# Which partitions four reads fill, and which keys a block transpose takes, in the wide cross attentions of a decoder kernel

## The chip, the cores and the metric

The kernel runs on one core of one Trainium2 chip. The time is the device time of one execution in microseconds (us). Three runs of the kernel before took 2110.76, 2118.01 and 2122.07 us; the median is 2118.01 us.

A core has five engines that run side by side, each with its own instruction queue: TensorE (PE in the profile; PEld is its weight loads), VectorE (DVE), ScalarE (ACT), GpSimd (POOL) and SyncE (SP), which here only issues DMA transfers. 16 DMA engines move the data of all queues. Working memory on the core has 128 partitions (rows); matrix products come out in eight banks.

## The reference

Four layers of a decoder over x of 4 batches, 256 tokens and 128 features, with a context of 512 tokens and 96 features. Each layer is self-attention, cross-attention and a feed-forward part. The change touches two of these twelve parts, the cross-attentions of the first and the last layer, with 16 heads of 64 features each:

```python
q = query @ w_q                      # 256 tokens x 1024
k, v = jnp.split(context @ w_kv, 2, axis=-1)   # 512 keys x 1024 each
scores = jnp.einsum('bhqd,bhkd->bhqk', q, k) * SCALE
attn = jax.nn.softmax(scores, axis=-1)
out = jnp.einsum('bhqk,bhkd->bhqd', attn, v)
return out.reshape(B, NQ, INNER) @ w_out + b_out
```

The first layer's version adds low-rank terms to the weights and treats the last 4 of the 512 context tokens apart. All is in 32-bit floats.

## The kernel before

The kernel calls the twelve parts by short names; X0 and X3 are the two cross-attentions, and F3, the last feed-forward part, is a local-attention network of six layers that fills the time from about 1,270 us on. Work of neighbouring parts is interleaved: the profile's stretches from 30 to 395 us and from 936 to 1270 us hold X0 and X3 with pieces of their neighbours.

Most of the order is not written out by hand. Every piece of work is registered with `op(name, ...)` under a name with an engine, a duration and a due time (a table, `NET`, with `"p_turn": ("DVE", 1.17, -1794.64)` among others), and with the buffers that it reads and writes. A planner (`Flow.order`) then plays the program through once with these numbers, at build time, and fixes the order of the instructions on every engine. On the chip each engine keeps to that order and waits, where it must, on semaphores. The numbers of the table are constants in the source.

X0 and X3 are made by `cross_wide` (lines 637 to 659) and `cross_pair` (661 to 724). A pair is two heads; there are 8 pairs in each of 4 batches, so 32 pairs in X0 and 32 in X3. For one pair:

- PE makes the keys (64 features of two heads by 512) and the queries, then, for each of two blocks of 128 queries, the scores of both heads: two banks of 128 queries x 512 keys (`p_scores`).
- DVE takes the row maximum of each (line 690), ACT the exponential with the row sum (line 692), DVE the reciprocal (line 694), POOL multiplies (line 697). The probabilities of a block lie in a tile `p` of 128 queries x 1024 (two heads x 512 keys).
- To weigh the values, PE needs the probabilities turned: keys on the partitions. This is done in two steps. First DVE transposes blocks of 32 x 32 inside `p` into a tile `ts` of 128 x 2048 (line 730, `blocks_turned`, name `p_turn`; once for each block of queries, so twice a pair). After it, partitions 32a to 32a + 31 hold, for the 32 queries of group a, the 32 keys of each block, one key to a partition.
- Second, the blocks have to come from the four groups of 32 partitions into their right places. `blocks_moved` (lines 735 to 745) sends `ts` to a room in HBM with one DMA of 1 MB (line 744, `p_send`, 128 rows of 8 KB) and reads it back with four DMAs of 256 KB (line 742, `p_move`), each of which collects from all four query groups what belongs to one quarter `m` of the key positions, in rows of 2 KB, and fills 32 partitions of the tile `pT`. Send and reads are issued by SP. SP waits for the turns before the send and for the landing of the send before the reads.
- PE multiplies with the values (`p_weigh`, line 718) and ACT copies the result out.

There are three rooms, two `ts`, two `pT` and three `p` tiles. SP also issues the fetches of weights (line 429) from the same queue, in the planned order. X0 differs in one thing that is seen in the profile: 508 keys are taken for the maxima and exponentials, and 4 are treated apart (line 707).

The key numbers of a block of 128 keys run from 0 to 127, and `pT` has key number n of a block on partition n.

Of the kernel before, what the change touches and what calls it, by code (L numbers as in the profile page):

```python
# [346 lines left out]
class Net:  # L347
# [378 lines left out]
    def blocks_turned(self, p, ts, t, reads):  # L726


        nc, done = self.nc, Buffer()
        self.op("p_turn", lambda: nc.vector.transpose(  # L730
            ts.t.rearrange("p (m t x i) -> p t m x i", m=4, t=2, i=32)[:, t],
            p.t.rearrange("p (x m i) -> p m x i", m=4, i=32)), reads, [done], [p, ts])
        return done

    def blocks_moved(self, ts, turned, pT):

        nc, room, sent = self.nc, self.fixed("room", self.rooms), Buffer()

        def move():
            from_, to = room.t.rearrange("(a j) (m x) -> m j a x", a=4, m=4), pT.t.rearrange("p (a x) -> p a x", a=4)  # L740
            for m in range(4):
                nc.sync.dma_start(out=to[32 * m : 32 * (m + 1)], in_=from_[m])

        self.op("p_send", lambda: nc.sync.dma_start(out=room.t, in_=ts.t), turned, [sent], [ts, room])
        self.op("p_move", move, [sent], [pT], [room])
# [2014 lines left out]
```

## Time and profile before

| | |
|---|---|
| time of the three runs | 2110.76, 2118.01, 2122.07 us |
| the profiled execution's own time | 2115.48 us |
| its span, first to last instruction | 2113.8 us |
| granted TensorE clock, mean | 0.974 of full speed |
| turns on DVE, line 730 | 128 of 1233 ns, 157.1 us |
| sends, line 744 | 64 of 1024 KB, 7.2 us from issue to landing (median) |
| reads, line 742 | 256 of 256 KB, 6.9 us from issue to landing (median) |
| DMA bytes in the whole run | 205.34 MB, of which sends and reads make 64 x 2 MB |

The page shows one execution. "Busy" is the time in which an engine works on an instruction; the rest is idle, and for every idle stretch the profile names what ended it ("PE bank L412 <- DMA arena<-room" is PE, at line 412, waiting for a transfer from a room into the working memory, whose name is `arena`). The chain is the sequence of work that ended last, followed back from the last instruction; only what lies on it sets the time directly. A table of stretches gives each engine's busy time in a piece of the span, the granted clock, the share of time for which the DMA engines were busy and the bytes that they moved.

### The profile page before, as it was taken

To read this page: it belongs to the slowest core of one execution; us is meant where nothing else is said; L and a number is where in the kernel's file an instruction comes from. 1 tells how busy PE (TensorE), PEld (TensorE's weight loads), DVE (VectorE), ACT (ScalarE), POOL (GpSimd) and SP (SyncE) were. 2 spreads that over 40 slices of the span, in tenths; PEclk is the share of its full clock that TensorE was granted. 3 is DMA by queue.
4 is the path that set the end of the run, shared out by engine and by line. 5 is a ranking of instruction groups with operands and counts; after the bars stand their busy time and mean duration, and the time that the engine had idled before them with its cause. 6 is when DMAs were issued, how large, how long until landed. Compare 5 with 4: busy or idle time off the path is not lost.

```text
span 2113.8 us, 58090 instructions
## 1 busy us (share of the span) xinstructions
PE 1974.5 (93%) x23506; PEld 1273.4 (60%) x23511; DVE 1659.4 (79%) x4177; ACT 1145.2 (54%) x2642; POOL 991.1 (47%) x1155
## 2 busy tenths in 40 slices
PE   9889999999999998998979889999999999999998
PEld 5445565766666675654544446666666666666566
DVE  6776877778775769898878579798798797987883
ACT  4554545254547676765536454555555556555553
POOL 4334334241221245544354355567476565674670
PEclk9999999999999999999989899999999999999999
DMA  5886828501100000029487872112112121021110
GB/s 162 235 252 197 234 77 243 161 21 45 69 9 9 1 1 26 25 66 249 126 209 238 234 215 82 42 32 84 31 53 72 32 63 52 24 83 33 29 43 22
DMA packets 79403, 205.34 MB, mean 97 GB/s; under 512 B 10648, under 2 KB 23008, under 8 KB 70944
## 3 DMA queue, kind: packets, MB, share of 16 engines
q1 hardware_dynamic: 66896, 185.72, 31.1%
q10 hardware_dynamic: 12240, 15.91, 2.5%
q8 instruction: 186, 3.05, 0.6%
q14 instruction: 81, 0.66, 0.1%
HBM read 108.80 MB, written 67.63 MB: 83 GB/s over the span
## 4 chain that ended last, share of the span: by engine, by line
PE 47%; DVE 26%; DMA 12%; POOL 7%; issue 4%; ACT 3%; SPq 1%; POOLq 0%; DVEq 0%; ACTq 0%
PE bank L412 30%; PE bank L1858 10%; DMA arena<-room 5%; DMA room<-arena 4%; PE bank L415 3%; DVE arena L2012 3%; POOL arena L2064 3%; DVE arena L2022 3%; DVE arena L2027 3%; PE bank L2074 2%; DVE arena L730 1%; DVE arena L2103 1%; DVE arena L2117 1%; DVE arena L690 1%; POOL arena L2026 1%
## 5 line engine op out<-in xcount | busy, mean ns | idle before, releaser
L412 PE MATMUL bank<-arena 128*128 128x128 f32 (+11 forms) x6824 | 884.0, 402 | 77.9 <-DMA arena<-room 55.4
L412 PEld LDWEIGHTS bank<-arena 32*128 32x128 f32 (+5 forms) x6824 | 543.0, 168 | 365.6 <-issue 152.1
L1858 PE MATMUL bank<-arena 64*64 64x32 f32 (+2 forms) x13584 | 648.2, 251 | 9.8 <-issue 4.9
L1858 PEld LDWEIGHTS bank<-arena 64*64 64x64 f32 (+2 forms) x13584 | 385.7, 127 | 207.1 <-issue 136.9
L420 ACT COPY arena<-bank 128x256 f32<-128x256 f32 (+4 forms) x498 | 223.4, 472 | 327.0 <-PE bank L412 273.2
L697 POOL TENSOR_SCALAR arena<-arena 128x508 f32<-128x508 f32 (+1 forms) x256 | 177.6, 701 | 229.2 <-DVE arena L694 223.9
L2026 POOL TENSOR_TENSOR arena<-arena 128x1024 f32<-128x1024 f32 x96 | 226.0, 2363 | 49.1 <-DVE arena L2012 46.9
L2064 POOL TENSOR_TENSOR arena<-arena 128x1024 f32<-128x1024 f32 x96 | 181.5, 1905 | 87.9 <-DVE arena L2048 87.9
L692 ACT ACTIVATE arena<-bank,arena 128x508 f32<-128x508 f32 (+1 forms) x256 | 173.8, 688 | 83.1 <-DVE arena L690 54.2
L690 DVE TENSOR_REDUCE arena<-bank 128x1 f32<-128x508 f32 (+1 forms) x256 | 164.2, 673 | 32.9 <-PE bank L412 32.8
L2107 POOL TENSOR_TENSOR arena<-arena 128x1024 f32<-128x1024 f32 x48 | 91.4, 1903 | 178.8 <-DVE arena L2104 153.7
L2022 DVE TENSOR_TENSOR arena<-bank,arena 128x512 f32<-128x512 f32 x192 | 127.3, 682 | 55.7 <-ACT arena L2020 50.6
L730 DVE STREAM_TRANSPOSE arena<-arena 128x1024 f32<-128x1024 f32 x128 | 157.1, 1233 | 17.5 <-DMA room<-arena 9.3
L1007 ACT ACTIVATE arena<-bank 128x512 f32<-128x512 f32 (+1 forms) x256 | 125.1, 579 | 66.1 <-PE bank L412 65.3
L2020 ACT ACTIVATE arena<-bank 128x512 f32<-128x512 f32 x192 | 111.5, 598 | 73.2 <-PE bank L1858 51.8
L415 PE MATMUL bank<-ident,arena 128*128 128x128 f32 (+2 forms) x733 | 125.9, 289 | 18.5 <-POOL arena L1656 4.9
L2012 DVE TENSOR_TENSOR arena<-bank,arena 128x256 f32<-128x256 f32 x384 | 138.2, 414 | 5.7 <-ACT arena L2020 5.1
L984 DVE TENSOR_REDUCE arena<-bank 128x1 f32<-128x512 f32 (+2 forms) x256 | 115.5, 516 | 34.0 <-PE bank L412 33.7
L415 PEld LDWEIGHTS bank<-ident,arena 128*128 128x128 f32 (+2 forms) x733 | 83.4, 143 | 80.8 <-issue 21.8
L2080 ACT COPY arena<-bank 128x512 f32<-128x512 f32 x192 | 105.2, 611 | 43.1 <-PE bank L2074 42.6
L2074 PE MATMUL bank<-ident,arena 128*128 128x128 f32 x768 | 105.0, 279 | 15.2 <-POOL arena L2064 15.2
L449 POOL TENSOR_TENSOR arena<-arena,neghalf 128x2 f32<-128x2 f32 (+1 forms) x56 | 42.9, 772 | 156.8 <-DVE arena L448 153.2
(229 smaller groups left out, 2524.8 us busy)
## 6 DMA issues: line engine op xcount, KB each, us to landing
room<-arena SPq DMA_DIRECT2D x64, 1024.0 KB, 7.2
arena<-room SPq DMA_DIRECT2D x256, 256.0 KB, 6.9
arena<-arena SPq DMA_DIRECT2D x48, 384.0 KB, 3.4
arena<-in_f_w SPq DMA_DIRECT2D x24, 512.0 KB, 5.9
arena<-in_f_wqkv ACTq DMA_DIRECT2D x18, 512.0 KB, 4.3
arena<-arena SPq DMA_DIRECT2D x48, 128.0 KB, 2.4
arena<-in_f_wo ACTq DMA_DIRECT2D x6, 512.0 KB, 4.3
arena<-in_f_w ACTq DMA_DIRECT2D x6, 341.0 KB, 3.0
```

The source lines that it names most:

```text
L412: self.nc.tensor.matmul(out, lhsT, rhs, start=start, stop=stop)
L415: self.nc.tensor.transpose(out, in_, self.d.ident)
L420: return self.op(name, lambda: copy(out(), in_()), reads, writes, holds)
L690: self.op("p_max", lambda ps=ps, one=one: nc.vector.tensor_reduce(one(nmx), ps.t[:, :n], AX.X, ALU.max, negate=True), [ps], [most], [nmx])
L692: self.op("p_exp", lambda ps=ps, one=one, cols=cols: nc.scalar.activation(cols(), ps.t[:, :n], AF.Exp, bias=one(nmx), accum_out=one(sums)) ...
L697: nc.gpsimd.tensor_scalar(cols(), cols(), one(sums), 1.0, ALU.mult, ALU.mult)
L730: self.op("p_turn", lambda: nc.vector.transpose(ts.t.rearrange("p (m t x i) -> p t m x i", m=4, t=2, i=32)[:, t], p.t.rearrange("p (x m i) ...
L1858: self.nc.tensor.matmul(out, lhsT, rhs, start=start, stop=stop)
L2012: nc.vector.tensor_mul(heads(tmp.t[:, cut])[:, :, lo : lo + 32], heads(ps.t)[:, :, 32 - lo : 64 - lo], spread(1, lo, lo + 32),)
L2022: op("cosine", lambda cut=cut, ps=ps: nc.vector.tensor_mul(heads(out.t[:, cut]), heads(ps.t), spread(0, 0, 64)), [ps, w["tab"]], [out])
L2026: op("rotary", lambda: nc.gpsimd.tensor_add(out.t, out.t, tmp.t), [out, tmp], [out])
L2064: nc.gpsimd.tensor_mul(heads(out.t), heads(out.t), rs.t[:, at : at + 16, None].to_broadcast([P, 16, 64]))
```

## The change

Within each block of 128 keys, key number n used to be written as n = 32 m + i, with m from 0 to 3 and i from 0 to 31. A 32 x 32 block transpose took the 32 neighbouring keys of one m, and read m went to the 32 neighbouring partitions 32 m to 32 m + 31. The change writes n = 4 j + m. A block transpose takes the 32 keys m, m + 4, m + 8 and so on, so its input is read at a step of four elements, and read m fills the partitions m, m + 4, m + 8 and so on up to m + 124. The tile `ts`, the room and the finished `pT` keep their shapes, and `pT` holds the same numbers in the same places. Counts, bytes and rows of the transfers are the same, and the planner's table is unchanged.

```diff
@@ blocks_turned
         self.op("p_turn", lambda: nc.vector.transpose(
             ts.t.rearrange("p (m t x i) -> p t m x i", m=4, t=2, i=32)[:, t],
-            p.t.rearrange("p (x m i) -> p m x i", m=4, i=32)), reads, [done], [p, ts])
+            p.t.rearrange("p (x j m) -> p m x j", m=4, j=32)), reads, [done], [p, ts])
@@ blocks_moved
             from_, to = room.t.rearrange("(a j) (m x) -> m j a x", a=4, m=4), pT.t.rearrange("p (a x) -> p a x", a=4)
             for m in range(4):
-                nc.sync.dma_start(out=to[32 * m : 32 * (m + 1)], in_=from_[m])
+                nc.sync.dma_start(out=to[m::4], in_=from_[m])
```

## The prediction

> **What bounds the kernel now.** I read the page first: its busy shares, the chain of work that ended last, and the DMA row of the slices.
>
> ```profile
> span 2113.8 us, 58090 instructions
> PE 1974.5 (93%) x23506; PEld 1273.4 (60%) x23511; DVE 1659.4 (79%) x4177; ACT 1145.2 (54%) x2642; POOL 991.1 (47%) x1155
> ...
> DMA  5886828501100000029487872112112121021110
> ...
> PE 47%; DVE 26%; DMA 12%; POOL 7%; issue 4%; ACT 3%; SPq 1%; POOLq 0%; DVEq 0%; ACTq 0%
> PE bank L412 30%; PE bank L1858 10%; DMA arena<-room 5%; DMA room<-arena 4%; PE bank L415 3%; DVE arena L2012 3%; POOL arena L2064 3%; DVE arena L2022 3%; DVE arena L2027 3%; PE bank L2074 2%; DVE arena L730 1%; DVE arena L2103 1%; DVE arena L2117 1%; DVE arena L690 1%; POOL arena L2026 1%
> ```
>
> TensorE is busy for 93%, but that average is not the answer: the DMA row is high in two places only. These are the two stages in which the change's instructions run. The table of stretches, cut at those stages (X0 from 30 to 395 us, X3 from 936 to 1270 us), shows who has room there. Columns: the stretch, busy us of each engine with its count of instructions, granted TensorE clock, DMA share, GB/s.
>
> ```profile
> core 0: us, PE busy (x) PEld busy (x) DVE busy (x) ACT busy (x) POOL busy (x), PEclk, DMA share, GB/s
> 30.00:395.00 365.00, 334.92 (x2117) 201.92 (x2115) 280.27 (x820) 182.74 (x498) 135.05 (x344) 0.96 0.72 204
> 936.00:1270.00 334.00, 287.26 (x1459) 153.90 (x1458) 260.44 (x581) 173.62 (x461) 152.89 (x187) 0.92 0.76 212
> ...
> 936.00:1000.00 64.00, 55.97 (x275) 28.27 (x271) 57.61 (x137) 36.58 (x103) 27.61 (x35) 0.95 0.89 247
> 350.00:400.00 50.00, 49.57 (x389) 36.78 (x389) 44.49 (x120) 14.29 (x39) 12.84 (x28) 1.00 0.87 219
> ```
>
> VectorE (DVE) is idle for 85 us of X0 and 74 us of X3: that is all the room a longer DVE instruction has there. Then two short stretches around one pair that had the DMA engines to itself: in the first only its send was moving, in the second nearly only its four reads. The SyncE timeline gives their issues.
>
> ```profile
> 1031.80:1034.40 2.60, 2.60 (x11) 1.11 (x8) 2.53 (x10) 1.48 (x5) 1.01 (x2) 1.00 0.93 384
> 1035.90:1041.70 5.80, 5.80 (x19) 1.79 (x17) 5.73 (x15) 4.89 (x14) 2.73 (x4) 1.00 0.97 232
> ```
> ```profile
> 1030.94 0.34 SPq L744 DMA_DIRECT2D room<-arena  x1
> 1034.93 1.73 SPq L742 DMA_DIRECT2D arena<-room  x4
> ```
>
> Same 1 MB, same queue, engines full both times (0.93 and 0.97), but the send to 128 neighbouring rows runs at 384 GB/s and the reads into 32 neighbouring partitions each at 232. Last, the rows of the turn and of the waits for the reads, from the answers for the line and the room:
>
> ```profile
> L730 DVE STREAM_TRANSPOSE arena<-arena x128: 1197/1235/1248, 36.9 to 1251.9; 128x1024 f32<-128x1024 f32 x128
> ```
> ```profile
> L742 SPq DMA_DIRECT2D arena<-room x256: 302/430/1622, 43.5 to 1270.0; - x128
> ...
>   PE bank L412: 57.3, 25
>   PEld bank L412: 11.1, 3
> ```
>
> TensorE stood still 28 times, 68.4 us in all, for a read that had not landed.
>
> **Part 1, the turns (line 730 to 732).** 128 of them, two a pair, same count and same output; only the input is now read four elements apart. Nothing in this trace shows DVE reading f32 from SBUF at such a stride. The full rate is known: reductions on line 984 take 683 ns for 512 elements and 284 ns for 128, so (683 - 284)/384 = 1.04 ns an element, and 1024 x 1.04 = 1.06 us of the turn's 1.233 us are elements. The low end is therefore +0: the turn already runs at one element per step and cannot gain. The high end: one more step for every element, +1.06 us, a turn of 2.30 us. I take the high end. Neither row decides; my reason is that the old pattern brings four wanted values in each 16 bytes and the new one brings one, so a reader that fetches more than 4 bytes at a time loses its neighbours. It is a choice, and its opposite is the first rival.
>
> [...]
>
> So DVE gets 128 x 1.06 = 136 us more work: 64 turns in X0, 280 + 68 = 348 us in a stage of 365; 63 in X3, 260 + 67 = 327 us in one of 334. Filled to 95% and 98%, DVE would bind both. It can't be packed that tightly, since its instructions wait in a fixed order for PE, ACT and POOL: in the two fullest long stretches with many turns it reaches 57.6/64 = 90% and 44.5/50 = 89%. At 90% X0 takes 348/0.90 = 387 us (+22) and X3 327/0.90 = 363 us (+29 to +30): **+52 us**. At 95% it would be +1.5 and +10 (**+12**), at 85% +45 and +51 (**+96**). What is late next: behind a turn on DVE stand the next pair's row maxima (line 690), for which ACT's exponentials wait (54.2 us today, "ACT arena L692 <- DVE arena L690"), which hold the banks that PE needs; and on SyncE the send behind the turn (185.5 us, "SPq L744 <- DVE arena L730"), with every later send and weight fetch behind it in that queue. The order of all engines is planned ahead from a weight for the turn that the change leaves alone, so nothing is rearranged for a longer turn. Between the stages DVE has 425 of 541 us busy but PE 523, so PE's delay isn't won back there.
>
> **Part 2, the four reads (line 742).** Same count, bytes and 2 KB rows, same place in SyncE's queue; 64 x 4 issues at 0.43 us stay as they are. Only the partitions written change. Ends: nothing gained (232 GB/s as now; 219 was the slowest such stretch, which would lose 0.3 us), and the send's 384 GB/s, the only row with the same bytes over all 128 partitions. 1.05 MB take 4.5 us at 232 and 2.7 at 384: -1.8 us a pair. I take that, being the nearest row in which the partitions are spread. A read lands 6.9 us after its issue (median), so 1.8 is 26%; of the 68.4 us for which PE stood waiting that is **-18 us**. The idle time of the turn's other side, send and fetches, shares the same engines and gains a little; I count it with the 90%.
>
> [...]
>
> **Sum**, against the profiled execution's own 2115.48 us (2.5 us below the median of the runs, inside their spread of 2110.8 to 2122.1): +52 - 18 = +34, so 2149.5, say **2150 us**, 1.5% slower. This case's own range runs from +12 - 18 to +96 with no help from the reads: 2110 to 2211.
>
> **The rivals.** 0.5%, about 10.6 us, is what a measurement of this kernel can tell from no change.
> 1. *The stride is free* (ends on the other side): turns stay at 1.233 us, the reads gain. [...] Gain: at least the 18 us. At most, all DMA time on the chain shrinks: in X0 the chain is 26% DMA of rooms (95 us), in X3 33% (111 us); the reads save 1.8 of a pair's 4.5 + 2.7 us, 25%, so 51 us. Midway: -35, **2080 us** (2064 to 2097). It decides if the turn's mean stays below about 1.5 us: with +0.27 us a turn DVE stays at 82% and 83% in the two stages.
> [...]
> 3. *The stride costs far more*, three extra steps an element, +3.2 us a turn: X0 (280 + 204)/0.9 = 538, X3 (260 + 201)/0.9 = 512: +351, **2467 us**. Nothing in the trace speaks for it but that a reciprocal (line 2104: 253 ns for 16 elements, 145 for one on line 694) shows 7 ns an element is possible.
> 4. *Neither price moves*: same rate in both, **2116 us**.
>
> **How the numbers follow.** Forecast 58%, rival 1 20%, rival 2 12%, rival 3 5%, rival 4 5%. The range must reach into rival 1: from 2075 to 2211 it leaves out rival 3, somewhat under half of rival 1 and the forecast's tails, some 17%. Faster by over 0.5%: nearly all of rival 1 and a few per cent of the forecast, 22%; within 0.5%: rival 4 and the low side of the forecast, 16%; slower 62%.
>
> **What would show it.** The turn's row (near 2.30 us, or 1.23); GB/s in a stretch with one pair's reads alone (near 384, or 232) and their landing (near 5 us, or 6.9); DVE's busy time in the two stages (near 348 and 327 us) and its idle time; PE's waits for reads (near 50 us). The part of the chain on lines 730 and 690 should grow and that of the reads shrink. The prediction is wrong if the turns keep their time, if PE's slack takes 136 us of DVE work without the stages growing, or if the reads' gain in a DMA-full stretch outweighs DVE there.

## The result, and the profile after

The changed kernel takes 2507.2 us (median of four runs, 2501.5 to 2507.8) against 2114.4 us for the kernel before on the same chip (four runs, 2108.0 to 2122.1): 1.185 times as long, with a 95% interval of 1.180 to 1.190. I had forecast 2150 us and a range of 2075 to 2211. The sign was right, the size and the cause were not. One execution of kernel F below took 3212.7 us at a granted clock of 0.603, against 2074.6 to 2084.6 us in its four others, and F's numbers leave it out. The profiled execution of the changed kernel has a span of 2504.7 us, and the instructions stand in the same order on every engine as before.

First the page of the changed kernel: instructions, busy time, the DMA row of the slices, the share of the DMA queue, and the shares of the chain that ended last, by engine.

```profile
span 2504.7 us, 58273 instructions
PE 2088.8 (83%) x23511; PEld 1313.6 (52%) x23511; DVE 1754.4 (70%) x4177; ACT 1144.1 (46%) x2642; POOL 988.4 (39%) x1155
...
DMA  4444342431110000104234244422121212111110
...
q1 hardware_dynamic: 66896, 185.72, 22.2%
...
PE 35%; DVE 31%; DMA 13%; POOL 7%; issue 5%; SPq 4%; ACT 2%; DVEq 0%; POOLq 0%; ACTq 0%
...
L730 DVE STREAM_TRANSPOSE arena<-arena 128x1024 f32<-128x1024 f32 x128 | 257.0, 2018 | 230.1 <-DMA arena<-room 213.4
...
arena<-room SPq DMA_DIRECT2D x256, 256.0 KB, 4.0
```

The rows of the queue and of the turn on the page before the change were:

```profile
q1 hardware_dynamic: 66896, 185.72, 31.1%
...
L730 DVE STREAM_TRANSPOSE arena<-arena 128x1024 f32<-128x1024 f32 x128 | 157.1, 1233 | 17.5 <-DMA room<-arena 9.3
```

Two things in the new page are what the prediction spoke of. A turn takes 2018 ns instead of 1233, 99.9 us more for the 128 of them, and DVE as a whole has 95 us more work (1754.4 against 1659.4). And the DMA engines need less time for the same 185.72 MB: 22.2% of 2504.7 us is 556 us, where 31.1% of 2113.8 was 657, so 101 us less, 1.6 us a pair. The third is new and far larger: just before the turns DVE stood still for 230.1 us, 213.4 of them until *reads from a room* had landed. Before the change that idle time was 17.5 us and no turn waited for a read. A turn doesn't use what a read brings; it reads `p` and writes `ts`, and the reads fill `pT`. There are 183 more instructions, although the program asks for the same work. Five are matmuls that the earlier trace lacks (23,506 against 23,511); counted in the two traces, the other 178 are semaphore instructions: 96 more on DVE, 53 on SyncE, 29 on the other three. The first line below is the turn's semaphore line before the change, the two after it the turn's answer in the changed kernel (durations in ns: least, median, most):

```profile
L730 DVEq EVENT_SEMAPHORE  x70: 21/21/50, 48.3 to 1248.0; - x70
```
```profile
L730 DVE STREAM_TRANSPOSE arena<-arena x128: 1944/2014/2162, 36.5 to 1639.5; 128x1024 f32<-128x1024 f32 x128
L730 DVEq EVENT_SEMAPHORE  x123: 21/50/6816, 48.1 to 1628.7; - x123
```

Before there were 70 of these semaphore instructions, none longer than 50 ns; now there are 123, and one lasts 6816 ns. Then, in the answer for the reads' line of the changed kernel, who waited for the reads (us in total, times):

```profile
L742 SPq DMA_DIRECT2D arena<-room x256: 577/604/1298, 48.7 to 1649.6; - x128
...
  DVE arena L730: 213.4, 34
  DVE arena L448: 63.7, 8
  ACT arena L2080: 23.5, 2
  POOL arena L2064: 21.0, 3
  DVE arena L918: 19.3, 3
...
  PE bank L412: 18.3, 7
```

Before, only TensorE waited for the reads (57.3 and 11.1 us in the lines of the prediction), apart from one wait of 0.8 us on GpSimd. Now it stands seventh: the turns wait most, and so do the statistics of a norm (line 448) and lines of the local-attention network (2064, 2080) whose data have nothing to do with a room. It goes the other way too. These are SyncE's waits, in us in total, times, and the longest, first one before the change and then two in the changed kernel:

```profile
SPq L744 <- DMA arena<-room: 53.4, 36, 5.9
```
```profile
SPq L744 <- DMA arena<-room: 161.7, 80, 5.4
...
SPq L742 <- DVE arena L694: 80.0, 12, 10.5
```

The reads (742) wait for reciprocals (694) that touch only small columns of sums, which ended none of their waits before, and the sends (744) wait for 161.7 us for reads, three times the 53.4 us of before. So a read has become a fence on both sides: it waits for work that it doesn't need, and work that doesn't need it waits for it. The chain of the changed kernel, in order of time, shows what this makes of a pair (start in us, duration in us):

```profile
157.33 2.00 DVE arena L730
159.35 3.83 DMA room<-arena
163.23 0.59 SPq L742
163.86 0.61 SPq L742
164.51 0.61 SPq L742
165.16 4.19 DMA arena<-room
169.38 0.05 DVEq L730
169.47 0.05 DVEq L730
169.57 0.09 DVE arena L730
```

Turn, send, issue of the reads, reads, next turn: one after the other, and nothing of another pair fills the gap: from 165.2 to 169.3 us, while the reads move, no compute engine works at all. The rooms, the two `ts` and the two `pT` tiles were there to let pairs overlap, and now they don't. The turns that ran from 36.9 to 367.4 us in X0 now run from 36.5 to 531.2 us (164 us longer), those of X3 over 524 us instead of 317 (207 longer): together 371 of the 391 us by which the span grew. The table of stretches of the changed kernel (columns as before) has the rest of the picture:

```profile
30.00:585.00 555.00, 396.59 (x2219) 229.47 (x2219) 331.66 (x828) 185.72 (x505) 138.23 (x351) 0.82 0.40 139
1100.00:1650.00 550.00, 360.72 (x1463) 179.31 (x1462) 324.40 (x616) 182.59 (x488) 159.15 (x196) 0.77 0.37 129
```

DVE is busy for 60% and 59% here, the DMA engines for 40% and 37%. Neither is the bound; both wait for each other. The granted TensorE clock fell to 0.82 and 0.77 (0.96 and 0.92 before), and PE's busy time rose from 1974.5 to 2088.8 us for the same matmuls: in these rows the PE that keeps stopping also has the lower clock. The transfer times of 3.9 us for a send (7.2 before) and 4.0 us for a read (6.9) are no gain by themselves: here each transfer has the engines nearly to itself, and in B below, where pairs overlap again, the same read takes 5.2 us.

### The profile page after: what moved, and what is told of

The parts are those of the page before. It is cut to its first block, busy times and chain, and to the rows that moved or that the text cites. A ratio compares the mean times of both kernels' runs of the same rounds, so it can differ in the third digit from the quotient of the medians.

```text
span 2504.7 us, 58273 instructions
## 1 busy us (share of the span) xinstructions
PE 2088.8 (83%) x23511; PEld 1313.6 (52%) x23511; DVE 1754.4 (70%) x4177; ACT 1144.1 (46%) x2642; POOL 988.4 (39%) x1155
## 3 DMA queue, kind: packets, MB, share of 16 engines
q1 hardware_dynamic: 66896, 185.72, 22.2%
## 4 chain that ended last, share of the span: by engine, by line
PE 35%; DVE 31%; DMA 13%; POOL 7%; issue 5%; SPq 4%; ACT 2%; DVEq 0%; POOLq 0%; ACTq 0%
PE bank L412 21%; DMA arena<-room 10%; PE bank L1858 9%; DVE arena L730 7%; SPq L742 4%; PE bank L415 3%; DVE arena L2012 3%; DMA room<-arena 3%; POOL arena L2064 2%; DVE arena L2022 2%; DVE arena L2027 2%; DVE arena L690 2%; PE bank L2074 2%; DVE arena L2103 1%; DVE arena L2117 1%
## 5 line engine op out<-in xcount | busy, mean ns | idle before, releaser
L412 PE MATMUL bank<-arena 128*128 128x128 f32 (+11 forms) x6824 | 945.6, 417 | 145.6 <-ACT arena L692 53.4
L412 PEld LDWEIGHTS bank<-arena 32*128 32x128 f32 (+5 forms) x6824 | 568.9, 175 | 478.8 <-issue 172.6
L730 DVE STREAM_TRANSPOSE arena<-arena 128x1024 f32<-128x1024 f32 x128 | 257.0, 2018 | 230.1 <-DMA arena<-room 213.4
L415 PE MATMUL bank<-ident,arena 128*128 128x128 f32 (+2 forms) x733 | 135.8, 303 | 128.5 <-DVE arena L459 52.2
L690 DVE TENSOR_REDUCE arena<-bank 128x1 f32<-128x508 f32 (+1 forms) x256 | 164.8, 679 | 12.2 <-PE bank L412 12.2
L412 PE MATMUL bank<-ctxT,arena 96*128 96x512 f32 (+2 forms) x168 | 93.2, 659 | 44.9 <-ACT arena L692 28.8
```

What stands on the lines that cost most here:

```text
L412: self.nc.tensor.matmul(out, lhsT, rhs, start=start, stop=stop)
L415: self.nc.tensor.transpose(out, in_, self.d.ident)
L690: self.op("p_max", lambda ps=ps, one=one: nc.vector.tensor_reduce(one(nmx), ps.t[:, :n], AX.X, ALU.max, negate=True), [ps], [most], [nmx])
L730: self.op("p_turn", lambda: nc.vector.transpose(ts.t.rearrange("p (m t x i) -> p t m x i", m=4, t=2, i=32)[:, t], p.t.rearrange("p (x j m) ...
```

## The experiments

The theory after these rows: the extra waits are false. All working tiles are pieces of one large tile, `arena`. Filling 32 neighbouring partitions of a piece was kept apart from its other pieces; filling every fourth partition is not, and each read is ordered against work anywhere in `arena`. The rival: the two edits' own prices (a turn 0.79 us longer, a read issue 0.60 us instead of 0.43 on SyncE) break the overlap and the waits are only where that shows. The two differ in what happens when `pT` gets tiles of its own and all else stays.

**A. Tiles of its own, kernel before (control).** The edit takes the two `pT` pieces out of `arena` (4096 of its columns) and makes two tiles of them, which the profile calls `turn`; the pieces behind them in `arena` move up. Line numbers and the planned order stay.

```diff
-        self.at |= at
-        self.arena = self.sb.tile([P, max(size, most)], F32, tag="arena", name="arena", bufs=1)
+        self.at = _layout(self.LAYOUT.replace(" pT ", " "), self.TILES)[0] | at
+        self.arena = self.sb.tile([P, size - 4096], F32, tag="arena", name="arena", bufs=1); self.turns = [self.sb.tile([P, 2048], F32, tag=f"turn{i}", name=f"turn{i}", bufs=1) for i in range(2)]
...
-        at, n = self.at[kind, i]
-        return self.arena[:, at : at + n]
+        at, n = self.at[kind, i] if kind != "pT" else (None, 0)
+        return self.arena[:, at : at + n] if n else self.turns[i]
```

> The kernel before, but the two pT tiles are tiles of their own and no longer pieces of the one large tile called arena; order, turns and reads as before. It is the control for the other kernels with pT of its own. All theories: 2116 us within 10, turns 1.23 us, reads 6.9 us from issue to landing, the waits as before.

Measured: 2112.9 us, 0.9997 times the kernel before (0.9983 to 1.0012). The tiles by themselves are worth nothing: the old pattern had no false waits to lose. It also settles a doubt: three pieces of the local-attention network lie on `pT`'s place in `arena`, and setting them apart from it gains nothing.

**B. Tiles of its own and the whole change.** Edit A, and the two lines of the change.

```diff
-            p.t.rearrange("p (x m i) -> p m x i", m=4, i=32)), reads, [done], [p, ts])
+            p.t.rearrange("p (x j m) -> p m x j", m=4, j=32)), reads, [done], [p, ts])
...
-                nc.sync.dma_start(out=to[32 * m : 32 * (m + 1)], in_=from_[m])
+                nc.sync.dma_start(out=to[m::4], in_=from_[m])
```

> The changed kernel, with pT in tiles of its own. Theory 1 (false waits: what places the semaphores takes a write to every fourth partition of a piece of the arena for a write to all of the arena, so the four reads wait for all work on it and all later work waits for them): the waits DVE L730 <- DMA arena<-room (213.4 us in the changed kernel) are gone, time 2090 to 2150 us. Theory 2 (load: the turns at 2.02 us instead of 1.23 fill DVE): still about 2500 us. Theory 3 (issue: a read takes SyncE 0.60 us to issue instead of 0.43, 45 us in all): about 2460 to 2500 us, since only the tile changes.

Measured: 2116.5 us, 1.0015 times the kernel before (0.9999 to 1.0031). Of the 393 us by which the medians differ all but 3 are gone, although every turn is still slow and every read still fills every fourth partition. The chain's shares, the turn and the reads on this kernel's page:

```profile
PE 41%; DVE 40%; POOL 8%; issue 5%; DMA 3%; ACT 3%; SPq 0%; POOLq 0%; ACTq 0%; DVEq 0%
...
L730 DVE STREAM_TRANSPOSE arena<-arena 128x1024 f32<-128x1024 f32 x128 | 260.4, 2045 | 10.7 <-POOL arena L699 7.9
...
turn<-room SPq DMA_DIRECT2D x256, 256.0 KB, 5.2
```

And the answer for its reads' line, the issues and then who waited for them:

```profile
L742 SPq DMA_DIRECT2D turn<-room x256: 577/603/2381, 44.7 to 1269.9; - x128
L742 SPq EVENT_SEMAPHORE  x70: 17/17/7099, 41.2 to 1262.8; - x70
...
  PE bank L412: 16.8, 8
  PEld bank L412: 7.8, 3
```

And SyncE's wait before the sends, for the reads:

```profile
SPq L744 <- DMA turn<-room: 12.2, 9, 3.7
```

The turn takes 2045 ns and its idle time is back to 10.7 us, none of it for a read of `pT`. Only TensorE waits for the reads, apart from three short waits of 1.9 us in all, and less than before. SyncE no longer waits for reciprocals before a read, the sends wait 12.2 us for reads instead of 161.7, and the page counts 58,094 instructions, so the extra semaphores are gone too. The issue on SyncE takes 603 ns as in the changed kernel, so that was not the cause either. The rival falls.

**C. The turns alone.** In the kernel before, only line 732 is changed; the reads stay as they were, so the keys come out in a wrong order.

```diff
-            p.t.rearrange("p (x m i) -> p m x i", m=4, i=32)), reads, [done], [p, ts])
+            p.t.rearrange("p (x j m) -> p m x j", m=4, j=32)), reads, [done], [p, ts])
```

> The kernel before with the turns' part of the change alone: transposes take every fourth key, reads fill 32 neighbouring partitions as before. The keys so stand in another order than the values that they weigh, so the output is not the reference's; work, bytes and order are the same. Theory 1: the turns take 2.02 us, 128 x 0.79 = 101 us more on DVE, which is 330 of 365 us in X0 and 310 of 334 in X3, about 90% and 93%; time 2116 to 2160 us. Theory 2: about 2500 us. Theory 3: 2116 to 2160 us.

Measured: 2143.1 us, 1.0146 times the kernel before (1.0126 to 1.0167), so +29 us for turns of 2034 ns (median; 1235 before). No compute engine waits for reads but TensorE (51.7 us in 20 waits, and 12.0 us in 3 of its weight loads), apart from three waits of at most 0.4 us. ACT's wait for the row maxima, which I had named as what is late next, is indeed the one that grows (54.2 us before):

```profile
ACT arena L692 <- DVE arena L690: 110.1, 62, 5.4
```

**D. The reads alone.** In the kernel before, only line 742 is changed.

```diff
-                nc.sync.dma_start(out=to[32 * m : 32 * (m + 1)], in_=from_[m])
+                nc.sync.dma_start(out=to[m::4], in_=from_[m])
```

> The kernel before with the reads' part of the change alone: transposes as before, each read fills every fourth partition. The keys stand in another order than the values that they weigh, so the output is not the reference's; work, bytes and order are the same. Theory 1: most of the loss, 2350 to 2480 us, turns at 1.23 us, and waits of DVE, PE, ACT and POOL for DMA arena<-room as in the changed kernel. Theory 2: no loss, 2065 to 2116 us, since the reads land faster. Theory 3: 45 us more on SyncE, at most 2160 us.

Measured: 2416.8 us, 1.1432 times the kernel before (1.1412 to 1.1451), +303 us, with turns that take no longer than ever. On its page:

```profile
span 2416.6 us, 58273 instructions
...
L730 DVE STREAM_TRANSPOSE arena<-arena 128x1024 f32<-128x1024 f32 x128 | 157.0, 1233 | 225.8 <-DMA arena<-room 215.7
```

The 58,273 instructions and the idle time before the turns (215.7 us for reads) are those of the changed kernel. The false waits come with this line of the change alone, and 303 of the 393 us with them.

**E. Tiles of its own, the reads alone.** Edit A and edit D. D and E differ in nothing but where `pT` lies.

```diff
+        return self.arena[:, at : at + n] if n else self.turns[i]
...
+                nc.sync.dma_start(out=to[m::4], in_=from_[m])
```

> pT in tiles of its own, reads to every fourth partition, turns as before the change. The keys stand in another order than the values that they weigh, so the output is not the reference's; work, bytes and order are the same. Against reads_alone (2416.8 us) only the tile of pT differs. Theory 1 (false waits): they were all of the loss of the reads' part, and what stays is its gain: between the kernel with own tiles and turned keys (2116.5 us) and the turns alone (2143.1 us) lie 27 us, so 2113 - 27 = 2086 us, 2070 to 2100. A theory by which the reads themselves cost the time (issue at 0.60 us, landing) has it above 2150 us.

Measured: 2062.8 us, 0.9773 times the kernel before (0.9752 to 0.9793), below the range that I had expected. Against D that is 354 us, and that is the price of the false waits with short turns, with all that follows from them. The reads themselves gain more than I had expected: 50 us, not 27. The shares of its chain, on the page:

```profile
PE 51%; DVE 28%; POOL 7%; DMA 5%; issue 5%; ACT 3%; SPq 1%; POOLq 0%; ACTq 0%; DVEq 0%
```

And two rows from the waits (us in total, times, longest), one of PE and one of SyncE, first in A and then here:

```profile
PE bank L412 <- DMA turn<-room: 61.7, 25, 6.7
...
SPq L742 <- DMA room<-arena: 147.3, 39, 10.9
```
```profile
PE bank L412 <- DMA turn<-room: 29.3, 13, 5.1
...
SPq L742 <- DMA room<-arena: 99.6, 28, 7.8
```

TensorE's waits at line 412 for reads fell from 61.7 us (in A) to 29.3, and SyncE's wait for the sends fell as well, from 147.3 us to 99.6. That the sends profit because they share the DMA engines with the reads fits but isn't shown: in C, with the reads as before, this wait was 109.8 us. DMA's share of the chain is 5%, where it was 12% on the page before the change.

**F. The reorder in the exponential, on the writing side.** The reads' gain without the slow turns: `p` holds the keys of each head already grouped by m, so that the turn reads neighbours. Here the exponential reads its bank straight through and writes key 4g + m of a head to column 128 m + g; the multiplication on line 697 takes a view to match. With edit A, and the reads of D.

```diff
-                cols = lambda p=p, e=e, lo=0, hi=n: p.t[:, e * NCTX + lo : e * NCTX + hi]
+                cols = lambda p=p, e=e, lo=0, hi=n: p.t[:, e * NCTX : (e + 1) * NCTX].rearrange("p (m g) -> p g m", m=4)[:, lo // 4 : hi // 4, :]
...
-                    cols(), ps.t[:, :n], AF.Exp, bias=one(nmx), accum_out=one(sums)), [ps, most], [prob], [p, sums, nmx])
+                    cols(), ps.t[:, :n].rearrange("p (g m) -> p g m", m=4), AF.Exp, bias=one(nmx), accum_out=one(sums)), [ps, most], [prob], [p, sums, nmx])
...
-            p.t.rearrange("p (x m i) -> p m x i", m=4, i=32)), reads, [done], [p, ts])
+            p.t.rearrange("p (e m x) -> p m e x", e=2, m=4)), reads, [done], [p, ts])
```

> As the kernel with own tiles and stepped reads, with the reference's output: the exponential on ACT writes key 4 g + m into column 128 m + g of its head, so that the turns read 32 neighbours and the keys end where the values want them. The step moves from DVE to ACT's writes and POOL's shares. If ACT pays nothing for steps of 128 elements in its writes: as the kernel with stepped reads and turns as before, 2070 to 2100 us. If it pays as the turn did (0.8 ns an element, 0.4 us on 256 exponentials of 0.69 us): 103 us more on an engine that is busy for 50% of X0 and X3, 2085 to 2130 us.

Measured: 2081.2 us (median of four runs, 2074.6 to 2084.6), 0.9862 times the kernel before (0.9839 to 0.9885).

**G. The same on the reading side.** As F, but the exponential reads the bank four columns apart and writes `p` straight through.

```diff
+                cols = lambda p=p, e=e, lo=0, hi=n: p.t[:, e * NCTX : (e + 1) * NCTX].rearrange("p (m g) -> p m g", m=4)[:, :, lo // 4 : hi // 4]
...
+                    cols(), ps.t[:, :n].rearrange("p (g m) -> p m g", m=4), AF.Exp, bias=one(nmx), accum_out=one(sums)), [ps, most], [prob], [p, sums, nmx])
```

> The same with the exponential reading the bank at a step of four and writing neighbours. If reading a bank at that step is free: 2070 to 2100 us. If it doubles the element's price (0.8 ns each, 0.4 us an exponential): 2085 to 2130 us.

Measured: 2062.6 us (2055.7 to 2066.3), 0.9765 times the kernel before (0.9739 to 0.9791), again below the expected range. This is the version that beats both kernels, by 51 us and by 445 us. Its page, the exponential and the turn:

```profile
L692 ACT ACTIVATE arena<-bank,arena 128x508 f32<-128x508 f32 (+1 forms) x256 | 174.0, 689 | 84.4 <-DVE arena L690 51.3
L730 DVE STREAM_TRANSPOSE arena<-arena 128x1024 f32<-128x1024 f32 x128 | 157.1, 1233 | 13.2 <-DMA room<-arena 5.6
```

Both have their old duration (688 and 1233 ns): the step of four is free where ACT reads a bank, so G keeps the whole 50 us of E. F, with the step of 128 columns where ACT writes, loses some 20 of them. Which of its instructions pays for that isn't shown.

**H. Two more steps for the turn.** In the kernel before, the first turn of each pair reads at a step of 2 elements (line 736 there) and the second at 8 (line 732); what is written no longer fits the reads. Each turn here also writes its 1024 columns in one piece, where the kernel before writes four pieces of 256; that was not varied by itself.

```diff
+            if t:
...
+                    p.t.rearrange("p (x j m) -> p m x j", m=8, j=32))
+            else:
...
+                    p.t.rearrange("p (x j m) -> p m x j", m=2, j=32))
```

> The kernel before, with turns that read at a step of 2 elements (8 bytes, first block of queries) and of 8 elements (32 bytes, second), each on a line of its own; counts and sizes the same. The turned numbers are then in a wrong order, so the output is not the reference's. If the price comes from 16 bytes that a reader fetches together: step 2 between 1.23 and 1.65 us, step 8 as step 4, 2.0 us. If it grows with the step: step 2 near 1.5, step 8 near 3.6 us. If any step costs the same: both 2.0 us.

Measured once: 2130.0 us, with these rows in its groups of instructions:

```profile
L732 DVE STREAM_TRANSPOSE arena<-arena 128x1024 f32<-128x1024 f32 x64 | 129.6, 2024 | 4.0 <-POOL arena L699 3.0 <-POOL arena L697 0.6
L736 DVE STREAM_TRANSPOSE arena<-arena 128x1024 f32<-128x1024 f32 x64 | 79.2, 1238 | 15.7 <-DMA room<-arena 11.4 <-POOL arena L699 2.8 <-POOL arena L697 1.3
```

Step 2 costs nothing (1238 ns against 1233), step 8 costs what step 4 does (2024 against 2018 to 2045). Between these steps the price is a jump, not a slope.

All of it in one table, in us by the medians (the kernel before: 2113 to 2114):

| | turns as before | turns at a step of 4 |
|---|---|---|
| `pT` with its own tiles, reads as before | 2112.9 (A) | not run |
| `pT` in `arena`, reads as before | 2113.7 (before) | 2143.1 (C) |
| `pT` with its own tiles, reads into every fourth partition | 2062.8 (E) | 2116.5 (B) |
| `pT` in `arena`, reads into every fourth partition | 2416.8 (D) | 2507.2 (after) |

## Why the prediction was wrong

**The step that failed** is the sentence of part 2, "Same count, bytes and 2 KB rows, same place in SyncE's queue; 64 x 4 issues at 0.43 us stay as they are. Only the partitions written change." I listed what the change removes and adds and wrote no new wait into the list, because the program's own buffers name none. The reads did bring waits, between tiles that share only the allocation: they cost 354 us with short turns (D less E), 391 with long ones (after less B). No rival had one. That the sign came out right is luck: slower was to come from the turns, and with the turns and reads of the change but without the false waits (B) the time hardly moves. That rival 3 gave 2467 us is chance too: its turns of 4.4 us don't exist.

What is shown is that the waits come with the pattern of partitions, and that a separate allocation of the tile written removes them. How the framework that places the semaphores decides what overlaps is not shown; that it takes the stepped write as touching all of `arena` is an inference from who waits.

**The issues** were wrong in the same sentence: 0.60 us instead of 0.43. In B and E, where it isn't mixed with other waits, SyncE stays under 2% of the chain.

**Part 1, the turn.** High end taken, and the end was right: 2.02 us, +0.79, where I had one more step per element, +1.06. My reason, a reader that fetches more than 4 bytes at a time and loses its neighbours, was a guess, and no run shows how DVE reads. H shows where the price sets in: 1238 ns at a step of 2 elements, 2024 ns at 8 (2018 at 4 in the changed kernel). The price is 0.79 us for 1024 elements, 0.77 ns each.

**The conversion to time.** With the measured price and my own 90%, X0 would take (280 + 64 x 0.79)/0.90 = 367 us (+2 to +3) and X3 (260 + 63 x 0.79)/0.90 = 344 us (+10), some +13 against my +52. C measured +29. So the term was too large by the size of the turn, and with the right size the filling limit would have been too small. My reading is that a longer turn also delays what stands behind it while DVE has room. That ACT's wait for the maxima comes next was right; it doubled, from 54.2 to 110.1 us in C. In B the stretches around the two stages show DVE as full as I thought possible:

```profile
30.00:395.00 365.00, 338.86 (x2132) 200.12 (x2130) 328.73 (x823) 181.48 (x498) 135.72 (x347) 0.97 0.59 206
936.00:1275.00 339.00, 293.80 (x1552) 151.61 (x1551) 311.26 (x588) 175.39 (x467) 156.33 (x188) 0.94 0.61 211
```

It is busy for 90% and 92% of them. The two effects don't add either: the turns cost 29 us with the old reads and 54 with the new ones (B less E), and the reads gain 50 us with short turns and 27 with long ones (C less B). With DVE as full as in B, the faster reads had less to give.

**Part 2, the reads' gain.** The direction was right and the size was not. The DMA engines save 1.6 us a pair (I had 1.8; 657 us of their time before, 556 after) and a read lands 5.1 us after its issue instead of 6.8 (E and A: 25%; I had 26%). One reading behind the 1.8 was wrong: the stretch at 232 GB/s did not hold "nearly only" the four reads. In its 5.8 us the engines moved 1.34 MB, and SyncE's timeline has the issue of the next send in it:

```profile
1038.53 0.34 SPq L744 DMA_DIRECT2D room<-arena  x1
```

Here is the stretch cut off before that send moves, and then one in the chain of the changed kernel above, where the four reads are alone and the engines as full:

```profile
1035.90:1040.30 4.40, 4.40 (x15) 1.47 (x13) 4.33 (x12) 3.63 (x11) 2.03 (x3) 1.00 0.94 209
```
```profile
165.90:168.10 2.20, 0.00 (x0) 0.00 (x0) 0.00 (x0) 0.00 (x0) 0.00 (x0) 1.00 0.95 347
```

So the reads ran at 209 GB/s and now run at 347, not quite the 384 that I had named as the sign. Why the spread partitions make them faster, no run shows.

What was mis-sized is the step from the landing to the time. I took a quarter off TensorE's waits, -18 us, and the whole gain was -50. A read that lands 1.7 us sooner takes up to 1.7 us off each wait, not a quarter of it: 25 waits of 2.5 us on average (A) became 13 of 2.3 us (E), 32 us less. The rest lies elsewhere, and I had priced nothing there. The bound of rival 1, a quarter of all DMA time on the chain, 51 us, is the same number, but not by its own argument: DMA's part of the chain more than halved, from 12% to 5% (before and E).

**Together**, had the waits not come, the change would have been worth +0.15% (B) where I had +34 us: the turns' cost and the reads' gain nearly cancel.

## What to carry to other kernels

When an access pattern changes, ask not only what it costs but with what the new pattern is ordered: here a stepped write into a piece of a big shared tile was ordered against work in its other pieces, and that cost 354 us (D less E). The signs were 178 more semaphore instructions for the same program and engines waiting for data that they don't read (213.4 us before the turns); giving the piece its own allocation was the test and the cure. And when a reorder is needed, put the step where its reader doesn't pay: here that was ACT reading a bank (689 ns, against 688 straight through), and it was worth 54 us against a turn on DVE (G and B).

## What the runs showed of the hardware that I had not expected

- DVE's block transpose of f32 from the working memory takes no longer at a step of 8 bytes (1238 ns in H, against 1233 for neighbours) and much longer, by nearly the same amount, at 16 and at 32 bytes (2018 ns in the changed kernel, 2045 in B; 2024 in H).
- ACT's exponential reads a bank at a step of four f32 in 689 ns (G), as fast as straight through (688 in the kernel before).
- Issuing a read of 256 KB on SyncE takes 603 ns (median, B and E) if it fills every fourth partition and 430 ns (the kernel before and A) if it fills 32 neighbours, with the same bytes and rows.
- Where PE stopped so often, the granted clock was lower as well: 0.82 and 0.77 in the two stages of the changed kernel, 0.96 and 0.92 before, and PE's busy time grew by 114 us for the same matmuls. Whether the stops alone lower the clock was not tried.
